# Graph transformer layer: the sort's two comparison rows are read from PSUM instead of SBUF

## The chip, the cores and the metric

The kernel runs on one core of a Trainium2 chip (trn2). The metric is device time in microseconds (us), as the median of several executions. A profile of one execution is at hand, with each engine's instructions: TensorE (PE, its weight loads PEld), VectorE (DVE), ScalarE (ACT), GpSimd (POOL) and SyncE, which only starts DMAs (SPq). Lines such as L363 are lines of the kernel before; the changed kernel has its lines from there on one further down (L364 for L363).

## The reference, cut to what matters

```python
xn = _layernorm(x)                                   # x: 6250 x 256
msgs = edge_weight[:, None] * xn[src_col]            # 100000 edges
gnn = segment_sum(msgs, row, num_segments=6250)
x = x + gnn + mix(xn)                                # Taylor attention, 8 heads
x = x + ffn(_layernorm(x))                           # 16 experts, top 2 of them
```

In the call, `values` is `edge_weight`, `row` is the input `src`, and `col` the input `dst`. The inputs come ordered by `dst`, so the sum into the 6250 rows needs the 100000 edges grouped by `src`. The change lies in that grouping and in nothing else.

## The kernel before, in words

The 6250 nodes are 49 blocks of 128 (`NT = 49`). The kernel first sorts the edges into 49 lists in DRAM, one for each block of `src` (two partial lists in each of two buffers `es_d`), then gathers the rows of `xn` edge by edge and adds them up with matmuls (L584, L588, L618) beside the first part of the attention, then does the rest of the attention, the routing and the experts, and the last layer norm.

The sort has 100 steps (`NS`) of 8 columns (`COLS`) of 125 edges (`EP`), and one loop with an order written out by hand (`manual_schedule`). Each engine takes its instructions in the order in which the loop emits them. A step consists of these parts:

- `hot(s)`: VectorE compares a row of block numbers 0 to 48 with the 8 block numbers of each partition (`binf`) and writes a one-hot `oh` of 8 x 49 in bf16 (L363). TensorE then makes from it, with triangular and all-one weights, each edge's place within its block, `rk` in PSUM (L369, L372). The row of block numbers is `iota`, an SBUF tile that GpSimd fills at the start; other parts of the kernel read it too.
- `cast(s)`: ScalarE copies `oh` to float32, `ohf` (L377).
- `counts(s)`: ScalarE copies the counts of the step out of `rk` (`crow`, L381), and TensorE adds them to the running counts `cum` in PSUM (L384).
- `place(s)`: VectorE reduces `rk` to `rank` (L389) and compares the rank with a row of 32 slots, 512 to 543, which gives `ohr`, 8 x 32 (L391). That row is `slot`, an SBUF tile (L301 to L303). Then `cr = ohr * rec` is made, with rec the edge's record (destination and weight): GpSimd has the first 5 columns of 8, VectorE the other 3 (L395). `ohr` has two buffers, `cr` three.
- `collect(s)`: 8 float32 matmuls of `ohf` and `cr` put the records of a block into a row of `ro`, in PSUM (L406).
- `evict(s)`: ScalarE copies `ro` out (L413) and works out where the rows go (`left` L416 and the index L417).
- `scatter(s)`: GpSimd starts an indirect DMA that writes the rows into the list (L422), to the two `es_d` in turn; each waits for the one before the last.

In the loop, step s emits in this order: counts(s-2), cast(s-1), collect(s-3), evict(s-4), the scatters, place(s-2), hot(s), and a piece of the layer norm: its statistics (`bst`, L250 and L251, on VectorE, in 49 of the steps), its root and its output `xo` (L459, on ScalarE, one tile to a step), and for each group of 4 tiles a store of `xo`, a store of the unchanged rows and a load of the next rows on SyncE's queue. On VectorE a step is thus rank, ohr, cr (3 columns), oh, and then statistics or small operations of the norm, if any. On GpSimd it is scatter and cr (5 columns). On TensorE it is cum, ro and rk. On ScalarE it is crow, ohf, the copy of ro, left, index, and xo, if any.

Ahead of the loop stand constants, among them `ident`, `before`, `owned` (the triangular weights, L300), and the values `base` and `live` for the index (L311 to L327). They are outside the hand-written order; the build puts them where they fit.

[...]In the sort, `rk` and `ro` have two buffers each, `cum`, `nbad` and, for the later gather, `agg` one each.

Of the kernel before, what the change touches and what calls it, by code (L numbers as in the profile page):

```python
# [9 lines left out]
F32 = mybir.dt.float32  # L10
# [4 lines left out]
ALU = mybir.AluOpType  # L15
# [4 lines left out]
P = 128  # L20
# [3 lines left out]
COLS = 8  # L24
RUN = 32
# [10 lines left out]
def gps_kernel(ctx: ExitStack, tc: tile.TileContext, x, src, dst, ew, wqkvT, bqkv, wprojT, bproj,  # L36
               temp, gate_w, gate_b, wpack, b2, gamma, beta, out):
    nc = tc.nc
# [8 lines left out]
    EP, EC = src.shape  # L47
    NT = (N + P - 1) // P
# [59 lines left out]
    def early(o, dtype=F32):  # L108
# [15 lines left out]
    iota = const.tile([P, P], F32, name="iota")  # L124
    nc.gpsimd.iota(iota, pattern=[[1, P]], base=0, channel_multiplier=0,
                   allow_small_or_imprecise_dtypes=True)
    pidx = const.tile([P, 1], F32, name="pidx")
    nc.gpsimd.iota(pidx, pattern=[[0, 1]], base=0, channel_multiplier=1,
                   allow_small_or_imprecise_dtypes=True)
# [24 lines left out]
    def weight_loads():  # L154
# [20 lines left out]
        if r0 < P:  # L175
# [22 lines left out]
                   allow_small_or_imprecise_dtypes=True)  # L198
    jlane = const.tile([P, CHL, WBUF], F32, name="jlane")
    nc.gpsimd.iota(jlane, pattern=[[1, CHL], [0, WBUF]], base=0, channel_multiplier=0,  # L200
                   allow_small_or_imprecise_dtypes=True)
# [5 lines left out]
                   allow_small_or_imprecise_dtypes=True)  # L207
# [5 lines left out]
                   allow_small_or_imprecise_dtypes=True)  # L213
# [48 lines left out]
    def features(f, once, ext, h0, r):  # L262
# [28 lines left out]
    sp = srt.enter_context(tc.tile_pool(name="sort", bufs=1))  # L291
    spp = srt.enter_context(tc.tile_pool(name="sort_p", bufs=1, space=PSUM))
# [4 lines left out]
    OWN = 512  # L297
    assert HC * EP <= OWN
    owned = sp.tile([P, P], BF16, name="owned")
    nc.vector.scalar_tensor_tensor(owned, ident, float(OWN), before, op0=ALU.mult, op1=ALU.add)  # L300
    slot = sp.tile([P, RUN], F32, name="slot")  # L301
    nc.gpsimd.iota(slot, pattern=[[1, RUN]], base=OWN, channel_multiplier=0,
                   allow_small_or_imprecise_dtypes=True)  # L303
    lneps = sp.tile([P, GRP], F32, name="lneps")
    nc.vector.memset(lneps, LN_EPS)

# [6 lines left out]
    base = sp.tile([P, 1], F32, name="base")  # L313
# [47 lines left out]
    def hot(s):  # L361
        oh = ohs[s % OHB]
        nc.vector.tensor_tensor(  # L363
            oh[:EP, :COLS * NT].rearrange("p (c b) -> p c b", b=NT),  # L364
            iota[:EP, None, :NT].to_broadcast([EP, COLS, NT]),
            binf[:EP, s * COLS:(s + 1) * COLS, None].to_broadcast([EP, COLS, NT]), op=ALU.is_equal)
        rk = spp.tile([P, COLS, NT], F32, name="rk", bufs=2)
        ohc = oh[:EP, :COLS * NT].rearrange("p (c b) -> p c b", b=NT)
        nc.tensor.matmul(rk, owned[:EP, :], ohc, start=True, stop=False, skip_group_check=True)  # L369
        rh, oh2 = (v.rearrange("p (h c) b -> p h c b", h=2) for v in (rk, ohc))  # L370
        for k in range(1, HC):
            nc.tensor.matmul(rh[:, :, k:, :], onesb[:EP, :], oh2[:, :, :HC - k, :],  # L372
                             start=False, stop=k == HC - 1, skip_group_check=True)
        rks[s] = rk
# [12 lines left out]
    def place(s):  # L387
        rs = rank[:EP, s * COLS:(s + 1) * COLS]
        nc.vector.tensor_reduce(rs, rks.pop(s)[:EP], AX.X, ALU.max)  # L389
        ohr = sp.tile([P, COLS, RUN], F32, name="ohr", bufs=2)  # L390
        nc.vector.tensor_tensor(ohr[:EP], slot[:EP, None, :].to_broadcast([EP, COLS, RUN]),  # L391
                                rs[:, :, None].to_broadcast([EP, COLS, RUN]), op=ALU.is_equal)
        cr = sp.tile([P, COLS, RUN, 2], F32, name="cr", bufs=3)
        for eng, a, b in ((nc.gpsimd, 0, GCOLS), (nc.vector, GCOLS, COLS)):
            eng.tensor_tensor(cr[:EP, a:b], ohr[:EP, a:b, :, None].to_broadcast([EP, b - a, RUN, 2]),  # L395
                              rec[:EP, s * COLS + a:s * COLS + b, None, :]
                              .to_broadcast([EP, b - a, RUN, 2]), op=ALU.mult)
        crs[s] = cr
# [82 lines left out]
    with tc.manual_schedule():  # L481
# [6 lines left out]
        for s in range(NS + 5):  # L488
            if s == 0:
                norm_load(groups[0])  # L490
                nc.vector.tensor_scalar(tmpi[:EP], srci[:EP], 7, None, op0=ALU.logical_shift_right)
                nc.vector.tensor_copy(binf[:EP], tmpi[:EP])
                hot(0)
                nc.vector.tensor_scalar(tmpi[:EP], srci[:EP], P - 1, None, op0=ALU.bitwise_and)
                nc.vector.tensor_copy(lanf[:EP], tmpi[:EP])
                nc.vector.tensor_copy(dstf[:EP], dstl[:EP])
                nc.vector.scalar_tensor_tensor(rec[:EP, :, 0], dstf[:EP], float(P), lanf[:EP], op0=ALU.mult,
                                               op1=ALU.add)
                nc.scalar.copy(rec[:EP, :, 1], ewf[:EP])
# [15 lines left out]
            if 0 <= s - 2 < NS:  # L515
                place(s - 2)
            if 0 < s < NS:
                hot(s)
# [316 lines left out]
    with tc.tile_pool(name="pw", bufs=2, space=PSUM) as pw:  # L835
# [24 lines left out]
        for hf in range(NF2):  # L860
# [10 lines left out]
            for j in range(NJ):  # L871
# [12 lines left out]
                                    op0=ALU.mult)  # L884
            c = KG0 + hf * (P + 1) + P
            nc.vector.tensor_scalar(wcol[:, 1, hf:hf + 1], gsum[:, NF2, c:c + 1], SCALE ** 2 / N, None,
                                    op0=ALU.mult)
# [272 lines left out]
    with tc.tile_pool(name="list", bufs=1) as lp, tc.tile_pool(name="list_p", bufs=1, space=PSUM) as lpp, \  # L1160
# [8 lines left out]
        base = lp.tile([P, NE], F32, name="base")  # L1169
# [28 lines left out]
        for c0 in range(0, NTP, BAT):  # L1198
# [8 lines left out]
            if c0 == 0:  # L1207
# [13 lines left out]
                same = lp.tile([P, CHM], F32, name="same")  # L1221
                nc.vector.tensor_tensor(same[:, WBUF:], ef[:, WBUF:], ef[:, :CHM - WBUF], op=ALU.is_equal)
                nc.vector.scalar_tensor_tensor(same[:, WBUF:], same[:, WBUF:], float(NE * P), ef[:, WBUF:],
                                               op0=ALU.mult, op1=ALU.add)
# [215 lines left out]
```

## Time and profile before

| what | value |
|---|---|
| median of 3 runs | 2060.29 us (2057.97 to 2068.98) |
| the profiled execution, its time | 2060.39 us |
| its span in the profile | 2058.6 us |
| mean granted TensorE clock | 0.885 |
| busy: TensorE, VectorE, ScalarE, GpSimd | 87%, 71%, 42%, 63% of the span |
| 100 `oh`, first and last start | 13.3 and 294.5 us |
| 100 `oh`, sum | 100.9 us |
| 100 `ohr`, sum | 43.5 us |
| 100 `cr` on GpSimd, sum | 83.1 us |
| 100 scatters on GpSimd, sum | 107.1 us |

In a page of the profile, the busy rows cut the span into 40 equal slices, and a digit is the busy share in tenths (9 is 90% or more); PEclk is the granted TensorE clock in tenths of full speed. A line of the timeline has start (us), duration (us), engine, line of the kernel, operation, output<-inputs, their shapes (partitions x elements) and types, and the count; in brackets at its end stand the time for which the engine sat idle before it and what ended that. Ends of one instruction and starts of the next on the same engine can overlap by some 0.07 us. A group line has the count, the busy time in us and the mean duration in ns.

### The profile page before, as it was taken

The page shows a single profiled execution, that of the slowest core. Times are in us where ns is not written, and L with a number is a line of the kernel's source. Part 1 is how long each engine was busy: PE and PEld are TensorE (multiplying, and loading weights), DVE is VectorE, ACT ScalarE, POOL GpSimd, SP SyncE. Part 2 cuts the span into 40 slices and gives each one's busy share as a digit, 9 for nine tenths or more (in the row PEclk, how much of TensorE's full clock was granted, in tenths as well). Part 3 has the DMA queues.
Part 4 walks back from the last instruction along what each step waited for, and adds up shares of the span by engine and source line. Part 5 has one row for each costly group of instructions (what it writes and reads, how often), then busy time and mean ns, then how long its engine had stood idle before and what let it go on. Part 6 is the DMA issues. An engine that isn't in the chain of part 4 may idle for free.

```text
span 2058.6 us, 36094 instructions
## 1 busy us (share of the span) xinstructions
PE 1794.0 (87%) x12126; PEld 1220.0 (59%) x12127; DVE 1468.7 (71%) x3775; ACT 873.9 (42%) x2487; POOL 1291.4 (63%) x1343
## 2 busy tenths in 40 slices
PE   4788877999999999699999999999849999999910
PEld 3555554665665666345555555555549999999910
DVE  6899987999999999256667667666654444444468
ACT  3666662232222322244444444444215555555523
POOL 4776765777777777376666666666525454554447
PEclk8555558999999999799999999999869999999955
DMA  5223225545545543333344444333342344323355
GB/s 176 86 84 96 75 81 143 169 137 184 155 136 159 175 155 104 82 100 111 112 121 111 120 117 118 112 112 105 95 166 73 113 148 145 117 78 134 86 206 180
DMA packets 144102, 256.19 MB, mean 124 GB/s; under 512 B 53856, under 2 KB 100393, under 8 KB 137642
## 3 DMA queue, kind: packets, MB, share of 16 engines
q0 software_dynamic: 55120, 145.94, 24.3%
q1 hardware_dynamic: 88534, 107.11, 16.3%
q8 instruction: 98, 1.61, 0.3%
q10 hardware_dynamic: 260, 0.80, 0.1%
q14 instruction: 90, 0.74, 0.1%
HBM read 314.99 MB, written 66.39 MB: 185 GB/s over the span
## 4 chain that ended last, share of the span: by engine, by line
PE 59%; DVE 28%; DMA 7%; issue 3%; ACT 1%; POOL 1%; SPq 0%; POOLq 0%; DVEq 0%; ACTq 0%
PE agg L618 14%; PE ph L1269 9%; PE py L1289 9%; DVE ft L267 6%; PE fp L926 5%; PE y L942 5%; DVE oh L363 4%; DMA msg<-xn_d,dsti 3%; DVE sel L588 3%; DVE rank L389 2%; PE pj L971 2%; DVE ohr L391 2%; PE gram L711 2%; DVE bst L250 2%; PE qkv L656 2%
## 5 line engine op out<-in xcount | busy, mean ns | idle before, releaser
L584 POOL DMA_INDIRECT msg<-xn_d,dsti x833 | 808.1, 970 | 359.7 <-PE agg L618 162.9
L618 PE MATMUL agg<-msg,sel 128*128 128x256 f32 x1666 | 454.1, 400 | 23.7 <-DMA msg<-xn_d,dsti 21.2
L618 PEld LDWEIGHTS agg<-msg,sel 128*128 128x128 f32 x1666 | 292.1, 191 | 220.4 <-issue 128.7
L909 ACT ACTIVATE sqf<-fp 128x512 f32<-128x512 f32 (+1 forms) x429 | 211.1, 575 | 256.1 <-PE fp L926 239.2
L588 DVE TENSOR_SCALAR sel<-iota,lane,wedge 128x128 f32<-128x128 f32 x833 | 257.5, 356 | 75.0 <-PE agg L618 71.6
L1269 PEld LDWEIGHTS ph<-xcT,wt 128*128 128x128 f32 x1808 | 273.9, 192 | 24.0 <-ACT xcT L1261 0.9
L1269 PE MATMUL ph<-xcT,wt 128*128 128x128 f32 x1808 | 276.1, 275 | 0.5 <-ACT xcT L1261 0.5
L1289 PE MATMUL py<-wt,hT 128*128 128x256 f32 x904 | 270.2, 381 | 2.6 <-DVE yc L1292 2.6
L1271 ACT ACTIVATE hT<-ph,wt 128x128 f32<-128x128 f32 x452 | 166.1, 368 | 195.9 <-PE ph L1269 194.5
L267 DVE TENSOR_TENSOR ft<-once,ext 128x2176 f32<-128x2176 f32 (+1 forms) x98 | 236.9, 2417 | 0.3
L1297 POOL DMA_INDIRECT ys_d<-yc,sidx x113 | 114.2, 1010 | 180.8 <-DVE yc L1292 74.2
L1292 DVE TENSOR_TENSOR yc<-py,xc 128x256 f32<-128x256 f32 x113 | 48.0, 425 | 199.4 <-PE py L1289 101.7
L1251 POOL DMA_INDIRECT xc<-ln_d,gidx x113 | 110.4, 977 | 90.2 <-DMA wt<-wp_d 52.4
L1289 PEld LDWEIGHTS py<-wt,hT 128*128 128x128 f32 x904 | 137.3, 192 | 3.5 <-ACT hT L1271 2.7
L422 POOL DMA_INDIRECT es_d<-acc x100 | 107.1, 1071 | 38.2 <-issue 6.9
L926 PE MATMUL fp<-hold,pair 32*128 32x512 f32 (+1 forms) x832 | 123.3, 618 | 0.0
L964 DVE RECIPROCAL rec<-rec 128x128 f32<-128x128 f32 (+1 forms) x98 | 82.9, 907 | 56.5 <-ACT rec L962 56.5
L711 PE MATMUL gram<-ft,vt 128*32 128x512 f32 (+2 forms) x1568 | 117.0, 415 | 4.1 <-DVE ft L267 4.1
L395 POOL TENSOR_TENSOR cr<-ohr,rec 125x320 f32<-125x320 f32 x100 | 83.1, 831 | 58.2 <-DVE ohr L391 44.9
L406 PE MATMUL ro<-cr,ohf 125*64 125x64 f32 x1600 | 111.7, 320 | 8.8 <-POOL cr L395 8.8
L942 PE MATMUL y<-sqf,wsq 128*32 128x512 f32 (+1 forms) x832 | 105.4, 578 | 0.0
L406 PEld LDWEIGHTS ro<-cr,ohf 125*64 125x64 f32 x1600 | 93.1, 221 | 15.4 <-POOL cr L395 10.4
(292 smaller groups left out, 2781.9 us busy)
## 6 DMA issues: line engine op xcount, KB each, us to landing
wt<-wp_d SPq DMA_DIRECT2D x113, 1154.0 KB
wp_d<-in_wpack SPq DMA_DIRECT2D x16, 1026.0 KB
msg<-xn_d,dsti POOLq DMA_INDIRECT x833
y<-ys_d SPq DMA_DIRECT2D x12, 1024.0 KB
xl<-in_x SPq DMA_DIRECT2D x12, 512.0 KB
xb_d<-xl SPq DMA_DIRECT2D x12, 512.0 KB
xn_d<-xo SPq DMA_DIRECT2D x12, 512.0 KB
acc<-xn_d SPq DMA_DIRECT2D x12, 512.0 KB
```

The lines of the kernel that those rows point to most:

```text
L267: nc.vector.tensor_tensor(bass.AP(tensor=f.tensor, offset=f.offset, ap=[[f.ap[0][0], r], [FW, HH], [D, ND], [1, D]]), bass.AP(tensor=o.ten ...
L406: nc.tensor.matmul(ro[64 * h:64 * h + 64], ohf[:EP, k * NT:k * NT + 64], cr[:EP, k].rearrange("p r f -> p (r f)"), start=c == 0, stop=c == ...
L584: nc.gpsimd.indirect_dma_start(out=m, out_offset=None, in_=xn_d, in_offset=bass.IndirectOffsetOnAxis(ap=dsti[:, b, o:o + 1], axis=0))
L588: nc.vector.tensor_scalar(s, iota, lane[:, b, o:o + 1], wedge[:, b, o:o + 1], op0=ALU.is_equal, op1=ALU.mult)
L618: nc.tensor.matmul(state["ps"], s, m, start=o == 0, stop=o == SUB - 1)
L711: nc.tensor.matmul(gram[h * D:(h + 1) * D, b, o:o + c1 - c0], vt[:r, hf * P + h * D:hf * P + (h + 1) * D], f[:r, h, c0:c1], start=False, s ...
L909: nc.scalar.activation(sq[:, :w], ps[:, :w], AF.Square)
L926: nc.tensor.matmul(ps[:, :w], pairf[h * D:(h + 1) * D, j * P:(j + 1) * P], G["q"][h * D:(h + 1) * D, hf, :w], start=True, stop=True)
L942: nc.tensor.matmul(y[h * D:(h + 1) * D, :w], wsq[:, hf, j, h * D:(h + 1) * D], f[h][:, :w], start=False, stop=j == NJ - 1, skip_group_chec ...
L1269: nc.tensor.matmul(ph, wt[:, k * FF + f * P:k * FF + (f + 1) * P], xT[:, k, :], start=k == 0, stop=k == KC - 1)
L1271: nc.scalar.activation(hTs[j][:, f, :], ph, AF.Relu, bias=wt[:, B1 + f:B1 + f + 1])
L1289: nc.tensor.matmul(py, hT[:, f, :], wt[:, W2 + f * C:W2 + (f + 1) * C], start=f == 0, stop=f == NF - 1)
```

## The change

The tile `slot` in SBUF goes, with GpSimd's iota that filled it. In its place a tile `same` of 49 + 32 float32 per partition lies in PSUM, in the pool of the sort (`spp`). VectorE fills its first 49 elements with a copy of `iota`, and the other 32 with `iota + 512`. `oh` and `ohr` read `same` as their first input instead of `iota` and `slot`; their second inputs, `binf` and `rank`, stay in SBUF. Nothing else is changed. In the order that is built, the two writes of `same` come ahead of the first `oh` on VectorE, and that `oh` comes behind `owned`; in the kernel before it came ahead of it.

```diff
@@ -298,9 +298,10 @@
-    slot = sp.tile([P, RUN], F32, name="slot")
-    nc.gpsimd.iota(slot, pattern=[[1, RUN]], base=OWN, channel_multiplier=0,
-                   allow_small_or_imprecise_dtypes=True)
+
+    same = spp.tile([P, NT + RUN], F32, name="same")
+    nc.vector.tensor_copy(same[:, :NT], iota[:, :NT])
+    nc.vector.tensor_scalar(same[:, NT:], iota[:, :RUN], float(OWN), None, op0=ALU.add)
@@ -362,7 +363,7 @@
         nc.vector.tensor_tensor(
             oh[:EP, :COLS * NT].rearrange("p (c b) -> p c b", b=NT),
-            iota[:EP, None, :NT].to_broadcast([EP, COLS, NT]),
+            same[:EP, None, :NT].to_broadcast([EP, COLS, NT]),
             binf[:EP, s * COLS:(s + 1) * COLS, None].to_broadcast([EP, COLS, NT]), op=ALU.is_equal)
@@ -388,7 +389,7 @@
-        nc.vector.tensor_tensor(ohr[:EP], slot[:EP, None, :].to_broadcast([EP, COLS, RUN]),
+        nc.vector.tensor_tensor(ohr[:EP], same[:EP, None, NT:].to_broadcast([EP, COLS, RUN]),
                                 rs[:, :, None].to_broadcast([EP, COLS, RUN]), op=ALU.is_equal)
```

## The prediction

> **What bounds the kernel now.** I read the page's slices first, to find where the two compared rows are used, then the timeline of that stretch, the groups by form, and the tile view of `oh`.
>
> ```profile
> PE   4788877999999999699999999999849999999910
> ...
> DVE  6899987999999999256667667666654444444468
> ...
> PEclk8555558999999999799999999999869999999955
> ```
>
> A slice is 51.5 us. The sort is slices 0 to 5: the `oh` instructions run from 13.3 to 294.5 us. VectorE (DVE) is busy at nine tenths there while TensorE stands at half clock. The sort ends before the first gather can start, so time saved in it comes off the span.
>
> ```profile
> 250.44 0.36 DVE L395 TENSOR_TENSOR cr<-ohr,rec 125x192 f32<-125x192 f32 x1
> 250.72 1.09 DVE L363 TENSOR_TENSOR oh<-iota,binf 125x392 bf16<-125x392 f32 x1
> 251.73 0.55 DVE L389 TENSOR_REDUCE rank<-rk 125x8 f32<-125x392 f32 x1
> 252.38 0.43 DVE L391 TENSOR_TENSOR ohr<-slot,rank 125x256 f32<-125x256 f32 x1
> 252.85 0.36 DVE L395 TENSOR_TENSOR cr<-ohr,rec 125x192 f32<-125x192 f32 x1
> 253.12 1.09 DVE L363 TENSOR_TENSOR oh<-iota,binf 125x392 bf16<-125x392 f32 x1
> 254.13 0.41 DVE L250 BATCH_NORM_STATS2 bst<-xl 128x6 f32<-128x256 f32 x1
> ```
>
> and beside it on GpSimd (POOL):
>
> ```profile
> 250.56 0.82 POOL L395 TENSOR_TENSOR cr<-ohr,rec 125x320 f32<-125x320 f32 x1 [0.82 <-DVE ohr L391]
> 251.54 1.15 POOL L422 DMA_INDIRECT es_d<-acc  x1 [0.16 <-issue]
> ```
>
> One step of the sort on VectorE: rank to ohr 0.65 us, ohr to cr 0.47, cr to oh 0.27, oh to the next instruction 1.01, together 2.40; a step with a layer-norm tile takes 0.55 more. No idle time is shown before any of these rows: VectorE is the bound. From 100 to 275 us 65 `oh` start, 2.69 us a step.
>
> Two things in `oh` matter. It reads 392 elements like the reduction in the row below, yet takes 1.09 us against 0.55. And GpSimd's share of `cr`, which reads two SBUF tensors, runs from 250.56 to 251.38. From 251.38 to the end of `oh` at 251.81 is 0.43 us, about 392 elements' worth: `oh` seems to have stood still until GpSimd was done. The start of the sort shows it more cleanly:
>
> ```profile
> 23.56 0.82 POOL L395 TENSOR_TENSOR cr<-ohr,rec 125x320 f32<-125x320 f32 x1 [3.45 <-DVE base L325]
> ...
> 23.71 0.68 DVE L327 SCALAR_TENSOR_TENSOR base<-live,base 128x1 f32<-128x1 f32 x1
> 24.32 0.55 DVE L363 TENSOR_TENSOR oh<-iota,binf 125x392 bf16<-125x392 f32 x1
> ```
>
> A one-element operation takes 0.68 us and ends at 24.39, just as GpSimd ends at 24.38; others of that size take 0.15. The `oh` behind it, with GpSimd free, takes 0.55. The tile view of `oh` gives minimum, median and maximum in ns:
>
> ```profile
> L363 DVE TENSOR_TENSOR oh<-iota,binf x100: 552/1087/1448, 13.3 to 294.5; 125x392 bf16<-125x392 f32 x100
> ```
>
> The 100 sum to 100.9 us; at 0.555 they would be 55.5. So 45 us of VectorE's time is standing behind GpSimd.
>
> **The change, part by part.**
>
> *Does the wait go?* After the change `oh` and `ohr` have one input in PSUM and one in SBUF. The trace has no two-input operation of that kind beside a GpSimd computation (`ft` at L267 is of that kind, 2407 to 2425 ns in 98 executions, but GpSimd only issues gathers beside it). It shows that operations with one input escape: a bst at 60.23 (0.41 us) lies wholly beside a `cr` of 59.77 to 60.88 and is not longer; so does a rank, always near 0.55. [...]I take 0.55: -0.53 us a step.
>
> *What does a PSUM input cost?* [...]The rows deny it: yc<-py,xc (PSUM and SBUF, 256 elements) has 425 ns and ohr (two SBUF, 256) 426; qk<-qkv,acc with 512 and a PSUM input is 683, pair<-ctr with 512 from SBUF 690; start to next start is 0.60 and 0.61. A row repeated out of PSUM, as here, costs nothing either: ft<-once,ext repeats its PSUM tile and has 2417 ns for 2176 elements, 1.04 ns for each beyond the 256 of ohr. I take 0, and 13 us for the range.
>
> *Setup.* GpSimd loses one iota (0.16 us, at 2.8 us, followed by memsets and zero stores that wait for DMA anyway). VectorE gains a copy and a tensor_scalar, some 0.15 to 0.22 each by the small rows of 14 us. The built order puts the first `oh` behind `owned` and the second row, at about 16 us instead of 13.3, so the first rank matmul starts 0.5 us later than its 15.95. The first `cast` waits for rec, which waits for edge weights landing near 20.7. Cover: 4 us. Cost nil; without the cover 0.5. On the other engines the order of instructions is otherwise unchanged, and the loop gains no wait.
>
> *What is late next.* On VectorE alone the step would be 2.69 - 0.53 = 2.16. Others need more.
> TensorE at half clock: rk to cum 0.93, cum to ro 0.20, ro 1.12, next rk at once: 2.27.
> Then a loop over two steps. oh(s), rk(s), cum, ScalarE's left, idx and xo, then crow(s), VectorE's rank(s), ohr, cr, oh(s+2). From starts in the trace: oh to rk 0.60 when not held; rk to cum 0.93; cum to left 0.33; left to idx 0.29; idx to xo 0.29; xo to crow 0.60; crow to rank 0.27; rank to oh 1.40. Sum 4.71, or 2.36 a step; without an xo 4.13, or 2.07. With `oh` as now the loop has 5.24, or 2.62, just hidden under 2.69. It can be seen where the statistics have run out:
>
> ```profile
> 293.10 0.55 DVE L389 TENSOR_REDUCE rank<-rk 125x8 f32<-125x392 f32 x1
> ...
> 295.94 0.57 DVE L389 TENSOR_REDUCE rank<-rk 125x8 f32<-125x392 f32 x1 [0.36 <-ACT crow L381]
> ...
> 298.34 0.57 DVE L389 TENSOR_REDUCE rank<-rk 125x8 f32<-125x392 f32 x1 [0.92 <-ACT crow L381]
> ```
>
> 298.34 - 293.10 = 5.24: two steps of that loop to the digit. So the next bound stands close behind. 48 of 100 steps have an xo: 0.48 x 2.36 + 0.52 x 2.28 = 2.32 a step, 0.37 saved of the 0.53. For the 81 steps from 80 us on: 30 us. In the 19 before them VectorE already waits (10.0 us for crow in all), so half of it: 3.5.
>
> *GpSimd* needs 0.74 + 0.16 + 1.01 + 0.03 = 1.94 a step when it catches up (76.68 to 78.63: 1.95). But each scatter waits for the landing of the one two before. Beside a burst of row stores and loads (152.10 to 154.10 on SyncE's queue) a scatter started at 152.23 lets the second after it start only at 158.14: 5.9 us for two steps, against 5.4 now and 4.7 then. So each of a dozen bursts makes GpSimd up to 1.2 us later than its step; it gains back 0.38 a step over the other six, and `cr`, which now ends at 251.38 for an ro of 253.01, keeps some 0.9 of these 1.6 us when two steps are 0.7 shorter. I charge 0.35 us a burst, 4 us; the ends are 0 and 12.
>
> Sum: 30 + 3.5 - 4 = 29.5. The profiled execution took 2060.39 us (span 2058.6 and 1.8 around it), as the median of the runs, 2060.29. Forecast 2060.4 - 29.5 = 2031. From the terms alone: 13 us of PSUM cost, at most half on the path, or 12 of landings give about 2045; fuller hiding 2016.
>
> **Rivals.**
> *All 45 us come off* (0.13): TensorE's idle 17% shrinks, it stays busy long enough for full clock, as from 24 to 32 us (clock 1.00 there), and rk to cum falls from 0.93 to 0.52; the loop is then 4.30, or 2.15, under VectorE's 2.16. Against it: 0.50 in every window from 40 to 300 us although TensorE was 82% busy, and GpSimd's landings. 2060.4 - 45 = 2015.
> *The wait stays* (0.09): the second SBUF operand, binf or the rank, is read where GpSimd's operands are, wherever the first lies. [...]For it: no row shows the mix beside GpSimd. It decides if `oh` is still over 1.0 us beside `cr`; slower than before as soon as the PSUM price is over 50 ns.
> *The wait only moves* (0.08): scatters wait for landings in most steps, or GpSimd's `cr` is now itself held; the step stays at 2.6: 2060 - 0.09 x 97 = 2052. Against: 1.94 against 2.32.
> The main case has 0.70.
>
> **Numbers.** A change under 0.5% (10.3 us) can't be told from none here. Faster: 0.70 + 0.13 and half of the last, 0.87; same 0.04; slower 0.09. Range 2011 to 2046: it holds the main case with its terms, and the full gain; left out are the two rivals of 0.17.
>
> **What would show it.** [...]An `oh` near 1.09 sinks the forecast; an `oh` at 0.55 with the step above 2.5 means that I mis-sized the coupling; 2.16 with a clock of 1.0 is the first rival.

## The result and the profile after

The changed kernel takes 2029.22 us, the median of 4 runs (2026.28 to 2037.44), against 2062.18 for the kernel before on the same chip (4 runs, 2057.97 to 2068.98): a ratio of 0.9843, with a 95% interval of [0.9803, 0.9884]. The profiled execution took 2026.28 us with a span of 2024.4, 34.1 less than the one before. The last row store of the sort is issued at 270.79 us instead of 302.95, the first qkv product starts at 276.64 instead of 309.00. So 32.4 of the 34.1 us are gained in the sort. The forecast was 2031.

The page's slices of the kernel after (a slice is now 50.6 us):

```profile
PE   5789869999999996999999999999759999999900
...
DVE  6888869998999996466676667666654444444468
...
PEclk9665669999999998899999999999869999999955
```

VectorE is down to some eight tenths in the slices of the sort. TensorE's granted clock is no longer flat: in windows of 20 us from 60 to 260 us it is 0.50 in some and 0.59 to 0.70 in others. The tile view of `oh` after, in ns minimum, median and maximum:

```profile
L364 DVE TENSOR_TENSOR oh<-same,binf x100: 552/559/567, 15.4 to 262.9; 125x392 bf16<-125x392 f32 x100
```

All 100 are short now: they sum to 55.8 us instead of 100.9. None is left at 1.09. The regular stretch that was shown of before looks like this after (timeline of VectorE, about two steps):

```profile
167.22 0.56 DVE L364 TENSOR_TENSOR oh<-same,binf 125x392 bf16<-125x392 f32 x1
168.16 0.57 DVE L390 TENSOR_REDUCE rank<-rk 125x8 f32<-125x392 f32 x1 [0.38 <-ACT crow L382]
168.83 0.42 DVE L392 TENSOR_TENSOR ohr<-same,rank 125x256 f32<-125x256 f32 x1
169.29 0.36 DVE L396 TENSOR_TENSOR cr<-ohr,rec 125x192 f32<-125x192 f32 x1
169.57 0.56 DVE L364 TENSOR_TENSOR oh<-same,binf 125x392 bf16<-125x392 f32 x1
170.04 0.42 DVE L250 BATCH_NORM_STATS2 bst<-xl 128x6 f32<-128x256 f32 x1
...
170.59 0.55 DVE L390 TENSOR_REDUCE rank<-rk 125x8 f32<-125x392 f32 x1
...
171.98 0.56 DVE L364 TENSOR_TENSOR oh<-same,binf 125x392 bf16<-125x392 f32 x1
```

One step has idle time before `rank`, which waits for ScalarE's `crow`; the next has statistics and none. The two together take 171.98 - 167.22 = 4.76 us, where the prediction's loop over two steps had 4.71.

**Where VectorE's time went.** The groups by line from 20 to 300 us, count, busy us and mean ns, idle us before. First the kernel before:

```profile
L389 DVE TENSOR_REDUCE rank<-rk 125x8 f32<-125x392 f32 x100 | 55.2, 552 | 10.0 <-ACT crow L381 10.0
L395 DVE TENSOR_TENSOR cr<-ohr,rec 125x192 f32<-125x192 f32 x100 | 36.6, 366 | 3.4
...
L453 DVE TENSOR_TENSOR nb<-mvl,std 128x4 f32<-128x4 f32 x12 | 2.9, 242 | 0.4
L454 DVE TENSOR_TENSOR nb<-zeros,nb 128x4 f32<-128x4 f32 x12 | 2.9, 239 | 0.4
```

and the kernel after:

```profile
L390 DVE TENSOR_REDUCE rank<-rk 125x8 f32<-125x392 f32 x100 | 55.6, 556 | 14.6 <-ACT crow L382 14.3
L396 DVE TENSOR_TENSOR cr<-ohr,rec 125x192 f32<-125x192 f32 x100 | 39.3, 393 | 3.4
L454 DVE TENSOR_TENSOR nb<-mvl,std 128x4 f32<-128x4 f32 (+1 forms) x13 | 5.3, 406 | 0.4
L455 DVE TENSOR_TENSOR nb<-zeros,nb 128x4 f32<-128x4 f32 (+1 forms) x13 | 5.3, 404 | 0.4
```

Busy times of rows that overlap can't simply be added, so the sum is taken from the two timelines without overlap, from the start of the third `oh` to that of the last: 270.2 us before, 240.9 after, 29.3 less. In it `oh` gives 43.7 us and `ohr` 1.4. Taken back are 6.4 us of waiting in front of `rank` (5.9 to 12.3; the rest of the 10.0 and 14.6 above lies outside this stretch), 2.7 in `cr`, 4.4 in the two `nb`, and 2.2 in all other rows and waits. The loop thus gives 29.3 us; a further 2.3 us come from ahead of it, where the third `oh` starts at 22.00 instead of 24.32.

`cr` and `nb` still have two inputs in SBUF, and they still stand behind GpSimd. They now do it more often (`cr` is over 0.45 us 8 times of 100 instead of 2, `nb` over 0.25 us 15 times of 26 instead of 5), because GpSimd's `cr` is late more often. One such place, in the timeline after:

```profile
179.63 1.01 POOL L423 DMA_INDIRECT es_d<-acc  x1 [2.22 <-DVE bst L250]
180.67 0.73 POOL L396 TENSOR_TENSOR cr<-ohr,rec 125x320 f32<-125x320 f32 x1
...
180.88 0.74 DVE L396 TENSOR_TENSOR cr<-ohr,rec 125x192 f32<-125x192 f32 x1
...
181.45 0.80 PE L407 MATMUL ro<-cr,ohf 125*64 125x64 f32 x10 [0.65 <-POOL cr L396]
```

Row stores and a load had been issued on SyncE's queue at 172.66, 173.06 and 173.68. The scatter at 179.63 waited 2.22 us. The profile names `bst`, but a scatter needs nothing of `bst`; by the program what it needs from elsewhere is its rows, its index and the landing of an earlier scatter. That it was the landing is a reading here; the four lists below test it. GpSimd's `cr` then starts at 180.67, VectorE's `cr` beside it takes 0.74 instead of 0.36, and TensorE's `ro` waits.

### The profile page after: what moved, and what is told of

It reads as the page before. It is cut to its first block, busy times and chain, and to the rows that moved or that the text cites. A ratio compares the mean times of both kernels' runs of the same rounds, so it can differ in the third digit from the quotient of the medians.

```text
span 2024.4 us, 36094 instructions
## 1 busy us (share of the span) xinstructions
PE 1775.4 (88%) x12127; PEld 1208.9 (60%) x12127; DVE 1433.4 (71%) x3777; ACT 872.3 (43%) x2487; POOL 1281.1 (63%) x1342
## 4 chain that ended last, share of the span: by engine, by line
PE 61%; DVE 26%; DMA 6%; issue 3%; ACT 2%; POOL 1%; SPq 0%; POOLq 0%; DVEq 0%; ACTq 0%
PE agg L619 14%; PE ph L1270 10%; PE py L1290 10%; DVE ft L267 7%; PE fp L927 6%; PE y L943 5%; DVE sel L589 3%; DMA msg<-xn_d,dsti 3%; PE pj L972 2%; DVE rank L390 2%; DVE oh L364 2%; PE gram L712 2%; DVE bst L250 1%; DVE ohr L392 1%; PE y L939 1%
## 5 line engine op out<-in xcount | busy, mean ns | idle before, releaser
L423 POOL DMA_INDIRECT es_d<-acc x100 | 100.8, 1008 | 42.2 <-issue 7.8
L407 PE MATMUL ro<-cr,ohf 125*64 125x64 f32 x1600 | 103.2, 302 | 12.2 <-POOL cr L396 12.2
L657 PE MATMUL qkv<-acc,xT 128*128 128x512 f32 (+1 forms) x196 | 93.9, 602 | 4.8 <-ACT xT L259 3.2
```

## The experiments

Each ratio is against the kernel before, run beside it on the same chip, with a 95% interval in brackets. "Step" is the mean from the start of the third `oh` to that of the last, 97 steps: 2.785 us before, 2.483 after.

### Which of the two rows, and which input

**Only `oh`'s row in PSUM**; the slots are in SBUF, filled by GpSimd's iota, as before. The edit is against the kernel before.

```diff
+    same = spp.tile([P, NT], F32, name="same")
+    nc.vector.tensor_copy(same, iota[:, :NT])
...
-            iota[:EP, None, :NT].to_broadcast([EP, COLS, NT]),
+            same[:EP, None, :NT].to_broadcast([EP, COLS, NT]),
```

> Only the row of block numbers (read by oh) lies in PSUM; the slot row stays in SBUF as before. Theory (oh stood behind GpSimd's cr because both its inputs were in SBUF; ohr was not held): oh near 0.56 us, the sort as short as in the changed kernel, so 2029 to 2034 us; scatters on GpSimd back from 1.01 to a mean near 1.07. Rival (both rows are needed, or the gain comes from what else moved, such as GpSimd's iota that is gone and the order of the first instructions): oh short, but clearly less than 30 us gained, 2040 or more.

2032.54 us (2029.39 to 2033.37), 0.9858 [0.9831, 0.9885]. `oh` sums to 55.6 us; step 2.505. This is the whole gain within the intervals. The scatters have a mean of 1.014 us, not 1.07 as expected.

**Only the slots in PSUM**; `oh` reads `iota` again. The edit is against the changed kernel.

```diff
-            same[:EP, None, :NT].to_broadcast([EP, COLS, NT]),
+            iota[:EP, None, :NT].to_broadcast([EP, COLS, NT]),
```

> Only the slot row (read by ohr) lies in PSUM; oh reads iota in SBUF as before. Theory: oh stays near 1.09 us, ohr 0.43 us as ever, scatters near 1.01 us because no two-input SBUF operation lies beside their second half; VectorE remains the bound, so 2056 to 2062 us. Rival (ohr's place matters, through GpSimd's scatters): a gain of 10 us or more.

2064.27 us (2057.61 to 2071.72), 1.0008 [0.9988, 1.0028]. The groups by line of this kernel, 20 to 300 us:

```profile
L363 DVE TENSOR_TENSOR oh<-iota,binf 125x392 bf16<-125x392 f32 x98 | 103.6, 1057 | 0.0
...
L391 DVE TENSOR_TENSOR ohr<-same,rank 125x256 f32<-125x256 f32 x99 | 42.0, 425 | 11.9 <-POOL cr L395 1.5 <-DVE rank L389 0.5
```

`oh` is held as before. `ohr` was hardly ever held (100 sum to 43.5 us before, at 425 ns each they would be 42.5), so its half of the change buys nothing. The scatters stay at 1.075 us, where 1.01 was expected: their lengthening went away with `oh`'s row and not with `ohr`'s, against what I had expected. Why is not settled.

**The inputs swapped**: SBUF first, PSUM second, in both.

```diff
-            same[:EP, None, :NT].to_broadcast([EP, COLS, NT]),
-            binf[:EP, s * COLS:(s + 1) * COLS, None].to_broadcast([EP, COLS, NT]), op=ALU.is_equal)
+            binf[:EP, s * COLS:(s + 1) * COLS, None].to_broadcast([EP, COLS, NT]),
+            same[:EP, None, :NT].to_broadcast([EP, COLS, NT]), op=ALU.is_equal)
...
```

> The changed kernel with the two inputs of oh and of ohr swapped: first the SBUF one, second the PSUM one. Theory (what counts is that at most one input lies in SBUF): oh 0.56 us, ohr 0.43 us, 2027 to 2035 us. Rival (it is the first input that is read where GpSimd reads): oh near 1.09 us again and about 2060 us.

2031.73 us, 0.9848 [0.9819, 0.9876]. Tile view:

```profile
L364 DVE TENSOR_TENSOR oh<-binf,same x100: 547/553/561, 16.1 to 262.3; 125x392 bf16<-125x392 f32 x100
```

Which of the two inputs lies in PSUM makes no difference to the wait here: the longest of the 100 is 561 ns, against 567 with the first input in PSUM and 1448 with both in SBUF.

### The wait taken away without PSUM

**In the kernel before, VectorE makes all 8 columns of `cr`**, so GpSimd computes nothing in the loop; both rows stay in SBUF.

```diff
-        for eng, a, b in ((nc.gpsimd, 0, GCOLS), (nc.vector, GCOLS, COLS)):
+        for eng, a, b in ((nc.vector, 0, COLS),):
```

> The kernel before (all rows in SBUF), but VectorE makes all 8 columns of cr and GpSimd none. Theory (GpSimd's cr is what oh waits for): oh 0.56 us with both inputs in SBUF; cr 0.69 us on VectorE (0.36 for 192 elements, 512 now); a step of 2.69 - 0.53 + 0.33 = 2.49 us, so some 19 us less, about 2041 us. Rival (oh is slow by itself, from reading repeated rows out of SBUF): oh stays at 1.09, the step grows to 3.0 us, about 2090 us.

2028.01 us (2026.28 to 2029.56), 0.9832 [0.9804, 0.9859]. Tile view:

```profile
L363 DVE TENSOR_TENSOR oh<-iota,binf x100: 554/558/612, 13.6 to 271.3; 125x392 bf16<-125x392 f32 x100
```

With two SBUF inputs and no computation beside it on GpSimd (its scatters still run), `oh` takes 558 ns: so GpSimd's `cr` was the cause, and 559 from PSUM is the price without a surcharge. `cr` grows to 0.69 us, and the step is 2.55, from 100 to 250 us as over all 97, where 2.49 was expected. The last row store of the sort starts at 279.0, 23.9 us earlier than before and 8 later than with the change. That the whole time is nevertheless no longer than with the change comes in the main from behind the sort: from the first qkv to the first fp product it took 544.3 us, against 548.3 before, 550.5 after, and 549.8 to 553.1 in the three kernels above. I have no explanation for that spread, and it limits what whole times of different kernels can tell here to some 9 us.

### What the two next limits cost

Two limits stood in the prediction behind the removed wait: the loop through ScalarE over two steps, and the landings of the scatters.

**ScalarE's work for `evict` emitted ahead of `counts`**, on the changed kernel.

```diff
+            if 0 <= s - 4 < NS:
+                evict(s - 4)
             if 0 <= s - 2 < NS:
                 counts(s - 2)
...
-            if 0 <= s - 4 < NS:
-                evict(s - 4)
```

> The changed kernel with evict(s-4) emitted ahead of counts(s-2) instead of behind collect(s-3), so that on ScalarE left and the index no longer wait for the cum of the same step, and xo no longer stands between cum and the next crow. Theory (with oh short, a regular step of 2.38 us is the loop oh, rk, cum, left, index, xo, crow, rank, ohr, cr, oh of 4.71 us over two steps): the loop falls to 4.1 us, TensorE's 2.27 us a step is next, the regular steps become 2.27 to 2.30 us, less waiting of rank for crow, and the last oh starts 5 to 8 us earlier than at 262.9. Rival (the landings of the scatters set the pace): nothing changes, last oh at 262 to 264 us.

2065.06 us, 1.0002 [0.9985, 1.0018]; step 2.825. The expectation failed: the gain of the change is gone altogether, with `oh` still at 558 ns. Timeline of this kernel:

```profile
181.34 1.12 PE L407 MATMUL ro<-cr,ohf 125*64 125x64 f32 x16
...
182.51 0.21 ACT L414 COPY acc<-ro 128x64 f32<-128x64 f32 x1 [0.96 <-PE ro L407]
...
183.33 0.24 ACT L382 CAST crow<-rk 32x98 bf16<-32x98 f32 x1
...
183.60 0.56 DVE L390 TENSOR_REDUCE rank<-rk 125x8 f32<-125x392 f32 x1
```

The copy of `ro` is part of `evict`. Put ahead of `crow`, it makes ScalarE wait for TensorE's `ro`, and `crow` and `rank` queue behind it. The waits of this kernel from 20 to 275 us (total, times, longest) show it as the largest:

```profile
ACT acc L414 <- PE ro L407: 86.0, 87, 3.3
```

I had moved a waiting instruction to the front of ScalarE's queue without pricing the wait.

**Four lists instead of two**, on the changed kernel, so that a scatter waits for the one four before.

```diff
-    es_d = [dram.tile([2 * NROW], F32, name=f"es{i}_d") for i in range(2)]
+    es_d = [dram.tile([2 * NROW], F32, name=f"es{i}_d") for i in range(4)]
...
-        e = es_d[s % 2]
+        e = es_d[s % 4]
```

> The changed kernel with four buffers for the scattered lists, taken in turn, so that a scatter waits for the landing of the fourth before it and not the second. The two added buffers are neither zeroed nor read, so half of the edges' records are left out of the result, and only the sort's own length is to be compared. Theory (bursts of row stores make scatters late): the idle stretches of 1.2 to 2.9 us before a scatter, once in some eight steps, are gone, the mean step falls from 2.46 to about 2.38 us and the last oh starts 6 to 9 us earlier than at 262.9. Rival (the landings are hidden by the slack of cr): less than 2 us.

The two added lists are neither zeroed nor read, so half of the records are missing behind the sort, and only the sort is compared. The last `oh` starts at 251.87, 11.0 us earlier than after; step 2.361. Groups by line, 20 to 300 us, first the scatters of the changed kernel, then this one:

```profile
L423 POOL DMA_INDIRECT es_d<-acc x100 | 100.8, 1008 | 42.2 <-issue 7.8 <-DVE ohr L392 6.8 <-ACT left L417 5.1
```

```profile
L423 POOL DMA_INDIRECT es_d<-acc x100 | 100.7, 1007 | 19.0 <-issue 11.0 <-ACT crow L382 2.4 <-ACT xo L460 2.4
...
L396 DVE TENSOR_TENSOR cr<-ohr,rec 125x192 f32<-125x192 f32 x100 | 36.7, 367 | 3.4
```

GpSimd's idle time before the scatters was 42.2 us after and is 19.0 here. VectorE's `cr` is back at the 36.6 us of before, and the two `nb` at 5.4 together: what they were held falls away with the landings.

**Both edits together**, `evict` ahead of `counts` and four lists:

> Both edits together: evict ahead of counts, and four buffers for the lists (half of the records left out of the result). Theory: with the loop and the landings out of the way TensorE's 2.27 us a step is the bound; a mean step of 2.28 to 2.32 us and the last oh at 244 to 249 us. If one of the two alone was the bound, it is the same as that one.

Step 2.755, last `oh` at 289.7. It fails for the reason of the first: ScalarE again stands in front of the copy of `ro`, for 80.9 us from 20 to 275 us.

**The same four lists on the kernel before:**

> The kernel before with four list buffers, of which two are neither zeroed nor read: half of the records are left out of the result, and only the sort's length counts. In the changed kernel the same edit took 0.12 us off the mean step (2.48 to 2.36). Theory (the landings were mostly covered when VectorE needed 2.69 us a step): 0 to 0.05 us off the mean step of 2.785, last oh at 290 to 294.5 us. Rival (the landings cost as much before as after, so they are no part of why the gain was 0.30 and not 0.53 us a step): 0.12 us off, last oh near 283 us.

Step 2.773 against 2.785, last `oh` at 292.4. So landings cost the kernel before 0.012 x 97 = 1.2 us, and the changed one 0.122 x 97 = 11.8. The change made 10.6 us of them visible, by one trace of each of the four kernels. Scatters and `oh` from 20 to 300 us, in the kernel before:

```profile
L422 POOL DMA_INDIRECT es_d<-acc x97 | 104.1, 1073 | 33.5 <-issue 6.9 <-ACT acc L417 5.2 <-ACT crow L381 4.5
L363 DVE TENSOR_TENSOR oh<-iota,binf 125x392 bf16<-125x392 f32 x98 | 99.8, 1018 | 0.0
```

and with four lists on it:

```profile
L422 POOL DMA_INDIRECT es_d<-acc x98 | 107.0, 1092 | 20.6 <-issue 8.6 <-ACT acc L417 6.8 <-ACT crow L381 2.8
L363 DVE TENSOR_TENSOR oh<-iota,binf 125x392 bf16<-125x392 f32 x99 | 104.7, 1058 | 0.0
```

GpSimd thus stood in front of its scatters idle for 33.5 us in the kernel before too, not much less than the 42.2 after. With the landings out of the way VectorE waited less elsewhere, but each `oh` was held longer (1058 ns against 1018), and the step stayed. That, as far as these traces tell, is how the landings were hidden.

**Only the index ahead of `counts`**: `left` and the index move, the copy of `ro` stays.

```diff
+        runs[s] = run
+
+    def index(s):
         idx = idxb[:, s % RUNB:s % RUNB + 1]
         left = sp.tile([P, 1], F32, name="left", bufs=4)
...
-        runs[s], idxs[s] = run, idx
+        idxs[s] = idx
...
+            if 0 <= s - 4 < NS:
+                index(s - 4)
             if 0 <= s - 2 < NS:
                 counts(s - 2)
```

> The changed kernel with evict split: only left and the index of step s-4 go ahead of counts(s-2); the copy of ro stays behind collect. In the run before this one the copy went ahead too, and ScalarE stood 91 us in front of it. Theory of the loop, once more: without xo between cum and crow it has 4.1 us over two steps; steps of 2.35 us fall to TensorE's 2.27 or below, steps with statistics stay at VectorE's 2.41, so the mean step falls by 0.03 to 0.08 us, the last oh to 255 to 260 us, the time to 2020 to 2027. Rival (the loop is not what holds the steps without statistics, but the landings are): last oh at 262 to 264. If left in front costs ScalarE a new wait, slower.

Beside this kernel and the next two, the kernel before took 2208.41 us. In their traces the stage from the first qkv to the first fp product takes some 635 us instead of 550; why is not known. The sort is not longer. So ratios and the sort's own times are compared. This kernel took 2175.3 us, 0.9854 [0.9813, 0.9896]. Timeline of VectorE, one step:

```profile
168.27 0.56 DVE L364 TENSOR_TENSOR oh<-same,binf 125x392 bf16<-125x392 f32 x1
168.74 0.56 DVE L390 TENSOR_REDUCE rank<-rk 125x8 f32<-125x392 f32 x1
169.40 0.42 DVE L392 TENSOR_TENSOR ohr<-same,rank 125x256 f32<-125x256 f32 x1
169.86 0.36 DVE L396 TENSOR_TENSOR cr<-ohr,rec 125x192 f32<-125x192 f32 x1
170.14 0.56 DVE L364 TENSOR_TENSOR oh<-same,binf 125x392 bf16<-125x392 f32 x1
```

This step without statistics takes 1.87 us with no idle time in it; in the changed kernel the same step, the one shown from 167.22 to 169.57, takes 2.35: the loop was there, and this edit opens it. From 100 to 250 us the mean step is 2.35 against 2.44, a little better than expected. Yet over all 97 it is only 2.471 and the last `oh` starts at 262.8, not at the 255 to 260 expected. The loss lies mostly in the first 30 steps, and the largest piece of it is one scatter behind a burst of stores and loads issued at 57.91 to 58.95 us:

```profile
67.44 1.01 POOL L426 DMA_INDIRECT es_d<-acc  x1 [5.26 <-DMA es_d<-acc]
```

The same scatter stood 2.89 us in the changed kernel, and the step there is 2.07 us shorter. So a landing takes back a good part of what the loop gives; whether it would be as long in another execution, one trace can't show.

**The layer norm's stores and loads spread**, on the changed kernel: one tile to a step instead of four at once, the same bytes.

```diff
-        rows_dma(nc.sync, xb_d, xg, g, True)
...
-        rows_dma(nc.sync, xn_d, xo, g, True)
+            nc.sync.dma_start(xn_d[t * P:t * P + r, :], xo[:r, i, :])
+            nc.sync.dma_start(xb_d[t * P:t * P + r, :], xg[:r, i, :])
...
+                if t + GRP < NT:
+                    u = t + GRP
+                    nc.sync.dma_start(lns[u - u % GRP][0][:rows_of(u), u % GRP, :],
+                                      x[u * P:u * P + rows_of(u), :])
```

> The changed kernel with the row stores and loads of the layer norm split by tile: each tile's two stores go out as soon as its xo is written, and each tile of the next group is loaded when the same tile of this group has its statistics, in place of three transfers of 512 KB in a row. Same bytes, no list buffer added. Theory (bursts make scatters late): most of the 11 us that four list buffers took off the sort; steps of 3.0 to 3.6 us at the bursts fall to 2.4 to 2.6; last oh at 253 to 258 us, 2017 to 2024 us. Rival (scatters are late by their own number, or the more numerous transfers delay them): last oh at 262 us or later.

2163.15 us, 0.9815 [0.9768, 0.9862]; step 2.389, last `oh` at 255.2. GpSimd's idle time before scatters falls from 42.2 to 28.7 us. So most of what the landings cost (0.094 us a step of 0.122) comes from the bursts, not from the number of bytes.

**Index and spread together**, which leaves nothing of the reference out:

> Both edits that keep the whole result: index ahead of counts, and stores and loads split by tile. Theory: the gains add as far as VectorE (about 2.2 us a step) and TensorE (2.27) allow: mean step 2.30 to 2.36 us, last oh at 246 to 253 us, 2012 to 2020 us, faster than both kernels. If it is no faster than the better of the two alone, they remove the same wait.

2158.92 us, 0.9772 [0.9738, 0.9805]; step 2.362, last `oh` at 251.7. Its ratio is below that of the change alone (0.9843, run at another time; the intervals barely touch) and its sort ends 11 us earlier. This version is faster than the kernel before beside it by 49.5 us, where the change alone gave 33.0 beside its own; from the spread alone (0.9815) its interval doesn't part it.

**Index and four lists** on the changed kernel, one execution:

> The changed kernel with index ahead of counts and four list buffers (two neither zeroed nor read, so half of the records are left out of the result; only the sort's length counts). Four buffers alone gave a mean step of 2.361 us and the last oh at 251.9 us, 41 of the 45 us by which the oh became shorter. Theory (the loop through xo holds back the other 4 us): mean step 2.30 to 2.33 us, last oh at 246 to 250 us. Rival (what remains lies elsewhere, such as in TensorE's 2.27 us or the first twenty steps): no more than 1 us off, last oh at 251 us or later.

Step 2.337, last `oh` at 250.0, against 251.87 with four lists alone. Measured from the third `oh` the index gives 2.3 us once landings are out of the way: the loop cost about half of the 4 us that I had put it at by then.

## Why the prediction came out right

By its own steps:

- **The wait goes: right.** `oh` takes 0.559 us, as forecast, and not one of the 100 is held (maximum 567 ns). No row of before showed an operation with one input in PSUM and one in SBUF beside GpSimd's `cr`, so the 0.53 us a step rested on my choice between 0.55 and 1.09, with only one-input rows for it. The runs show the mix unheld in either order of the inputs: medians of 559 ns and, swapped, 553. The rival in which the wait stays is out. So are the two others: the sort ends 32 us earlier and not 45, and the step did not stay at 2.6.
- **A PSUM input costs nothing: right.** `oh` takes 559 ns from PSUM and 558 from SBUF with GpSimd quiet; `ohr` 425 and 424. The 13 us that I kept in the range for a PSUM input are shown by no run: these differences of 1 ns come to 0.2 us over the 200 instructions.
- **Setup: right in the sum.** The first rank matmul starts at 16.1 us instead of 15.9. The third `oh` starts 2.3 us earlier. Of this 1.7 us are hardly the change's: the first `ohr`, which waits for the edge weights, starts at 23.0 before, 21.3 after, and between 21.6 and 23.3 in the experiments, with either place of the rows. The other 0.6 us lie between that `ohr` and the third `oh`, where L327 was held before.
- **The step saved, 30 + 3.5 us: too small.** What failed is the rate of before. I put 65 `oh` into 175 us, 2.69 a step. There are 63, and from the first start to the last it is (272.8 - 102.1) / 62 = 2.75. The 2.32 forecast for the step after is met where landings are kept away: 2.33 over the last 79 steps with four lists. So some 0.43 a step was to be had, not 0.37. (Behind 80 us there are 78 `oh`, not 81, which would have taken 1 us off.) Without landings on either side the loop of steps is (2.773 - 2.361) x 97 = 40 us shorter, where I had 33.5.
- **What sets the 2.32 was half right.** VectorE alone would need not the 2.16 I gave but about 2.25: the rate was 2.75, and the mean `oh` from 100 to 240 us was 1.058 us, so 0.50 comes off and not 0.53. The loop over two steps exists (4.76 us against 4.71), but VectorE's steps with statistics, 2.41 each, fill most of the mean. And I took half clock for granted. After the change the clock is above 0.50 in part of the sort, and there some `ro` matmuls take 222 ns instead of 314. With four lists the step is 2.39 at a clock of 0.50 (202 to 243 us), 2.31 at 0.68 (103 to 161) and 2.25 at 1.00 (161 to 179), with `ro` medians of 314 ns in the first stretch and 222 in the last. So the 2.32 is met by a mean over clocks that the forecast did not have. For the changed kernel itself the clock explains little: 2.47 a step at 0.50 (159 to 216 us), 2.46 at 0.68 (82 to 119).
- **GpSimd's landings, 4 us: too small.** They take 10.6. The mechanism was named, but only TensorE's wait for `cr` was priced. The larger part goes another way: VectorE's own `cr` and `nb`, which keep two SBUF inputs, take 7.1 us more than before (2.7 and 4.4) behind a late GpSimd `cr`, and all but 1.3 of this is gone when both kernels have four lists. The wait that was removed from `oh` comes back there in small. The rest of the 10.6 is that landings shortened the holding of `oh` before and so cost little there.
- **L327, which I expected still at 0.68: wrong.** It is L328 now and took 0.15, because it ran at 21.61, ahead of GpSimd's `cr` at 21.85. An operation of its kind at 267.59 (L448, one element, two SBUF inputs) takes 0.68 beside a GpSimd `cr` of 267.44 to 268.26. That operation is still held; I had not seen that the order in time would change.
- **Nothing changed behind the sort, as I expected: right within what can be told.** It accounts for 1.7 us of 34.1. The last scatter is 32.3 us earlier, where I expected about 30.

Sum: the forecast had 33.5 from the steps less 4 for landings, 29.5. Measured are 40.0 less 10.6, 29.4, a start 2.3 us earlier, and some 2.4 us between the last `oh` and the end. Two terms were mis-sized by some 6.5 us each, in opposite directions. The mechanism was right; the accuracy of the total is luck.

Open are why the stage behind the sort varies by some 9 us between kernels that do the same there, what sets the clock, and why the scatters' own duration goes with `oh`'s row.

## What to carry to other kernels

Where a VectorE operation with two SBUF inputs takes much longer than others of its size, look for a two-input GpSimd computation that ends shortly before it does. Here one of VectorE's inputs in PSUM freed it (median of `oh` 1087 ns before, 559 after) at no price (558 with both in SBUF and no `cr` on GpSimd). Taking the work from GpSimd altogether is the other way: here it gave the same whole time, with a sort 8 us longer. Before counting a saving, take the rate of before from a first start to a last start, and list the other operations with two SBUF inputs on that engine: here `cr` and the two `nb` took 7.1 us more behind a late GpSimd `cr`. And ask what a faster loop runs into: here the scatters' landings beside bursts of stores, which cost 1.2 us before and 11.8 after, so that they took a quarter of the gain (10.6 of 40 us).

## What the hardware showed beyond that

In the kernel with only the slots in PSUM, the granted clock was recorded as 1.00 from 100 to 250 us, with matmuls of the same duration as under 0.50 in the kernel before: `ro` has a median of 314 ns in both. The tile views of `ro` in that window, before and with only the slots in PSUM:

```profile
L406 PE MATMUL ro<-cr,ohf x864: 314/314/370, 101.6 to 248.0; 125*64 125x64 f32 x173
```

```profile
L406 PE MATMUL ro<-cr,ohf x868: 314/314/370, 99.7 to 250.0; 125*64 125x64 f32 x174
```

The same holds from 100 us on in the kernel with `evict` first (mean clock 0.951). So the recorded clock is to be read beside a duration of TensorE: in the windows after where the record is above 0.50, some `ro` do take 222 ns.
